# Sparse attention and a routed feed-forward on one Trainium2 core: blank rows ahead of the experts' lists instead of behind them

## The chip, the cores and the metric

The kernel runs on one core of one Trainium2 chip. The metric is device microseconds of one execution. A core has five engines with queues of their own: TensorE (PE; its weight loads appear as PEld), VectorE (DVE), ScalarE (ACT), GpSimd (POOL) and SyncE (SP), which here only starts transfers. Semaphores order them.

## What is computed

4096 tokens of 512 features pass through graph attention with a sparse adjacency and then through a mixture of 8 experts, of which each token uses two:

```python
x = x + gnn(layernorm(x), adj, Wks, Wqs, Wvs, Wo)         # 8 heads of 64, masked by adj

def ffn(xf):                                              # xf = layernorm(x)
    logits = xf @ Wg + bg                                 # 8 experts
    topk_scores, topk_idx = top_k(logits, 2)
    topk_w = softmax(topk_scores)
    h = gelu(einsum('nd,edh->neh', xf, W1) + b1)
    y = einsum('neh,ehf->nef', h, W2) + b2
    sel = take_along_axis(y, topk_idx[:, :, None], axis=1)
    return sum(topk_w[:, :, None] * sel, axis=1)

x = x + ffn(layernorm(x))
```

The kernel computes an expert only for the tokens that chose it.

## The kernel before

It has three stages.

- **Stage 1** normalizes the tokens, computes keys, values and queries, and reads the adjacency in 32 blocks of 2 MB to list each query tile's neighbours.
- **Stage 2** does the attention over the listed keys. As groups of query tiles finish, it routes their tokens: each token's row (512 features, its number, two gates and a mark) is scattered to two places of `xs_d` in device memory. Expert `e` has the rows from `e * R` on, where `R = N + P`.
- **Stage 3** goes through 71 tiles (`NB`) of 128 rows (`P`). A tile belongs to one expert.

An expert's list is rarely a multiple of 128 rows long, so its last tile reads beyond the end of the list. Before the change, 128 blank rows are written behind each list once its length is known. A blank row carries zero features, zero gates and the number of a spare output row, `N + p`, so whatever comes out of it goes to a spare row.

Between stages 2 and 3 stands the arithmetic that makes the tile table, followed by the blank writes:

```python
def finish_routing(pool, psum, blank):
    pn = psum.tile([P, E], F32, name="pn")
    nc.tensor.matmul(pn, ones, count, start=True, stop=True)     # tokens of each expert
    many = pool.tile([P, E], F32, name="many")
    nc.vector.tensor_copy(many, pn)
    # ... tiles of each expert, and their running sum
    nc.vector.tensor_tensor(past, ..., op=ALU.is_ge)             # [P, NB, E]
    nc.vector.tensor_reduce(expert, past, axis=AX.X, op=ALU.add)
    nc.vector.tensor_mul(past, past, ...)
    nc.vector.tensor_reduce(first, past, axis=AX.X, op=ALU.add)
    # ... first: the row of xs_d at which each tile begins
    nc.vector.tensor_add(many, many, start_e)                    # the end of each list
    nc.vector.tensor_copy(table[:, :NB], expert[:1])
    nc.vector.tensor_copy(table[:, NB : 2 * NB], first[:1])
    nc.vector.tensor_copy(table[:, 2 * NB :], many[:1])
    nc.vector.tensor_add(first, first, number.to_broadcast([P, NB]))

    nc.sync.dma_start(out=xs_d[E * R : E * R + P, :], in_=blank)
    for e in range(E):
        last = nc.values_load(table[:, 2 * NB + e : ...], engines=(SP,), ...)
        s = nc.sync.dma_start(out=xs_d[bass.ds(last, P), :], in_=blank)
        # ... declared free of order against the scatters
```

Then comes a branch, taken past a slower general path that these inputs do not need (`again > 0` runs it). Behind the branch, stage 3 fetches the rows of a tile and the two bias rows of its expert, and works in a software pipeline:

```python
again = nc.values_load(redo, ...)
with tc.If(again > 0):
    ...                                                          # the general path

def fetch(b):
    e = nc.values_load(table[:, b : b + 1], engines=(SP, PE), ...)
    f = nc.values_load(table[:, NB + b : NB + b + 1], engines=(SP,), ...)
    r = work.tile([P, W], F32, tag="row", bufs=5)
    nc.sync.dma_start(out=r, in_=xs_d[bass.ds(f, P), :])
    bb = work.tile([P, 2, D], F32, tag="bb", bufs=4)             # b1 and b2, broadcast

def second(b):
    gate = ...                                                   # from the row's mark and gates
    # py = hT @ w2 on TensorE
    nc.vector.tensor_add(y, py, bs[b][:, 1])
    nc.scalar.mul(y, y, gate[:, 1:2])
    nc.gpsimd.indirect_dma_start(                                # adds y to rows of out
        out=out, out_offset=IndirectOffsetOnAxis(ap=r[:, D : D + 1].bitcast(I32), axis=0),
        in_=y, in_offset=None, compute_op=ALU.add)

for b in range(NB):
    if b + 4 < NB: fetch(b + 4)
    turn_hidden(b)          # PE transposes into pht
    hidden(b + 1)           # ph = xT @ w1, + b1, gelu
    turn(b + 2)             # PE transposes into pt_e
    second(b)
```

All 8 experts' `w1` and `w2` are in on-chip memory before stage 3 needs them. `w1` comes in during stage 2, `w2` in eight loads of 1 MB at its end.

Of the kernel before, what the change touches and what calls it, by code (L numbers as in the profile page):

```python
# [10 lines left out]
F32 = mybir.dt.float32  # L11
BF16 = mybir.dt.bfloat16
I32 = mybir.dt.int32
AF = mybir.ActivationFunctionType
ALU = mybir.AluOpType
AX = mybir.AxisListType
PSUM = bass.MemoryType.PSUM
DRAM = bass.MemoryType.DRAM

P = 128  # L20
# [12 lines left out]
def kernel(  # L33
# [31 lines left out]
    nc = tc.nc  # L65
    N, D = x.shape
    H, KD = Wo.shape[0], Wo.shape[1]
    E, _, HID = W1.shape
# [8 lines left out]
    SP, PE = mybir.EngineType.SP, mybir.EngineType.PE  # L77
    DIAG = math.exp(IDENTITY_BIAS)
    LOW, HIGH = 1e-25, 1e37
    R = N + P  # L80
    NB = (2 * N + E * (P - 1)) // P
# [5 lines left out]
    const = ctx.enter_context(tc.tile_pool(name="const", bufs=1))  # L87
# [5 lines left out]
    xs_d = dram.tile([E * R + P, W], F32, name="xs_d")  # L93
# [9 lines left out]
        out=below, in_=ones, pattern=[[1, P]], compare_op=ALU.is_gt, fill=0.0,  # L103
        base=0, channel_multiplier=-1,
    )
    number = const.tile([P, 1], F32, name="number")
    nc.gpsimd.iota(number, pattern=[[0, 1]], base=0, channel_multiplier=1,
                   allow_small_or_imprecise_dtypes=True)
# [13 lines left out]
    for r in range(1, 4):  # L122
        nc.vector.tensor_add(gather4, gather4, ident[:, r * Q4 : r * Q4 + E])
    start_e = const.tile([P, E], F32, name="start_e")
    nc.gpsimd.iota(start_e, pattern=[[R, E]], base=0, channel_multiplier=0,
                   allow_small_or_imprecise_dtypes=True)
    before = const.tile([P, E, E], F32, name="before")
    nc.vector.memset(before, 0.0)
    for e in range(1, E):
# [6 lines left out]
                   allow_small_or_imprecise_dtypes=True)  # L136
# [4 lines left out]
                   allow_small_or_imprecise_dtypes=True)  # L141
    full = const.tile([P, NT], F32, name="full")
    nc.gpsimd.iota(full, pattern=[[P, NT]], base=0, channel_multiplier=0,
                   allow_small_or_imprecise_dtypes=True)
    first = const.tile([P, NB], F32, name="first")
    table = const.tile([1, 2 * NB + E], I32, name="table")
    redo = const.tile([1, 1], I32, name="redo")
    blank = const.tile([P, W], F32, name="blank")
    nc.vector.memset(blank, 0.0)
    nc.gpsimd.iota(blank[:, D : D + 1].bitcast(I32), pattern=[[0, 1]], base=N,  # L150
                   channel_multiplier=1)
# [77 lines left out]
    ap = ap_cm.__enter__()  # L229
    with tc.tile_pool(name="wqkv", bufs=1) as wp, tc.tile_pool(name="p1", bufs=3) as work, tc.tile_pool(  # L230
        name="p1b", bufs=2
    ) as block, tc.tile_pool(name="lists", bufs=2) as lp, tc.tile_pool(
        name="ps1t", bufs=2, space=PSUM
    ) as ps_t, tc.tile_pool(name="ps1", bufs=3, space=PSUM) as ps, tc.tile_pool(
        name="ps1a", bufs=1, space=PSUM
    ) as ps_a, tc.tile_pool(
        name="ps1l", bufs=2, space=PSUM
# [11 lines left out]
        for n, src, queue in (("k", Wks, nc.scalar), ("v", Wvs, nc.scalar), ("q", Wqs, nc.sync)):  # L249
            for c in range(DC):  # L250
                queue.dma_start(out=w[n][:, c], in_=src[ts(c, P), :])
        nc.sync.dma_start(
            out=wo, in_=Wo.rearrange("h k o -> (h k) o").rearrange("(c p) o -> p c o", p=P)
# [9 lines left out]
            out=step, in_=ones, pattern=[[1, P]], compare_op=ALU.is_equal, fill=0.0,  # L263
            base=-1, channel_multiplier=-1,
        )

        other = lp.tile([P, NT], F32, bufs=1, name="other")
        part = lp.tile([P, NT], F32, bufs=1, name="part")
        nc.gpsimd.affine_select(
            out=other, in_=one_f, pattern=[[-P // NT, NT]], compare_op=ALU.is_ge,  # L270
# [3 lines left out]
            out=part, in_=one_f, pattern=[[P // NT, NT]], compare_op=ALU.is_gt,  # L274
# [4 lines left out]
                       allow_small_or_imprecise_dtypes=True)  # L279
        slot_of = lp.tile([P, NT], F32, bufs=1, name="slot_of")  # L280
        nc.gpsimd.iota(slot_of, pattern=[[P, NT]], base=P, channel_multiplier=1,
                       allow_small_or_imprecise_dtypes=True)
# [15 lines left out]
        adj_in, flags, base, row_x, started, rows_of = {}, {}, {}, {}, {}, {}  # L298
# [199 lines left out]
            load_x1(TPB + t)  # L498
        list_constants()
        nc.sync.dma_start(out=out[N : N + P, :], in_=blank[:, :D])  # L500

# [11 lines left out]
        for u in range(8 * NTB + 1):  # L515
            b, s = divmod(u, 8)
# [146 lines left out]
    scatters = []  # L663
# [10 lines left out]

    why = "computed from counts that sum to 2 N"

    def finish_routing(pool, psum, blank):

        pn = psum.tile([P, E], F32, name="pn")
        nc.tensor.matmul(pn, ones, count, start=True, stop=True)  # L680
        many = pool.tile([P, E], F32, name="many")
        nc.vector.tensor_copy(many, pn)
        more = pool.tile([P, E, NT], F32, name="more")
        nc.vector.tensor_tensor(
            more, many.unsqueeze(2).to_broadcast([P, E, NT]),
            full.unsqueeze(1).to_broadcast([P, E, NT]), op=ALU.is_gt,
        )
        tiles_e = pool.tile([P, E], F32, name="tiles_e")
        nc.vector.tensor_reduce(tiles_e, more, axis=AX.X, op=ALU.add)
        none = pool.tile([P, E], F32, name="none")  # L690
        nc.vector.memset(none, 0.0)
        upto = pool.tile([P, E], F32, name="upto_e")
        nc.vector.tensor_tensor_scan(
            upto, tiles_e, none, initial=0.0, op0=ALU.add, op1=ALU.add
        )
        past = pool.tile([P, NB, E], F32, name="past_e")
        nc.vector.tensor_tensor(
            past, nth.unsqueeze(2).to_broadcast([P, NB, E]),
            upto.unsqueeze(1).to_broadcast([P, NB, E]), op=ALU.is_ge,
        )  # L700
        expert = pool.tile([P, NB], F32, name="expert")
        nc.vector.tensor_reduce(expert, past, axis=AX.X, op=ALU.add)
        nc.vector.tensor_mul(past, past, tiles_e.unsqueeze(1).to_broadcast([P, NB, E]))
        nc.vector.tensor_reduce(first, past, axis=AX.X, op=ALU.add)
        nc.vector.tensor_sub(first, nth, first)
        nc.vector.tensor_scalar_mul(first, first, float(P))
        nc.vector.scalar_tensor_tensor(
            first, expert, float(R), first, op0=ALU.mult, op1=ALU.add
        )
        nc.vector.tensor_scalar_min(first, first, float(E * R))  # L710
        nc.vector.tensor_scalar_min(expert, expert, float(E - 1))
        nc.vector.tensor_add(many, many, start_e)
        nc.vector.tensor_copy(table[:, :NB], expert[:1])
        nc.vector.tensor_copy(table[:, NB : 2 * NB], first[:1])
        nc.vector.tensor_copy(table[:, 2 * NB :], many[:1])
        nc.vector.tensor_add(first, first, number.to_broadcast([P, NB]))

        nc.sync.dma_start(out=xs_d[E * R : E * R + P, :], in_=blank)
        for e in range(E):
            last = nc.values_load(  # L720
                table[:, 2 * NB + e : 2 * NB + e + 1], engines=(SP,), min_val=e * R,
                max_val=e * R + N, skip_runtime_bounds_check_because=why,
            )
            s = nc.sync.dma_start(out=xs_d[bass.ds(last, P), :], in_=blank)
            for t in scatters:
                tc.declare_no_dep(s.ins, t.ins, reason="other rows")
            scatters.append(s)


    w1_cm = tc.tile_pool(name="w1", bufs=1)  # L730
# [3 lines left out]
    with tc.tile_pool(name="p2a", bufs=2) as two, tc.tile_pool(  # L734
        name="p2o", bufs=1
    ) as single, tc.tile_pool(name="p3", bufs=2) as small, tc.tile_pool(
        name="ps_s", bufs=3, space=PSUM
    ) as ps_s, tc.tile_pool(name="ps_o", bufs=1, space=PSUM) as ps_o, tc.tile_pool(
        name="ps_k", bufs=1, space=PSUM
    ) as ps_k, tc.tile_pool(name="ps_e", bufs=2, space=PSUM) as ps_e:  # L740
        work_cm = tc.tile_pool(name="p2", bufs=4)
        work = work_cm.__enter__()
# [236 lines left out]
        for n, (i, c) in enumerate(items):  # L979
# [7 lines left out]
            if n >= 56 and n % 7 == 0 and loads:  # L987
                e, d = loads.pop(0)
# [43 lines left out]
        nc.tensor.matmul(pf[:1], least, ones32[:, :1], start=True, stop=True)  # L1032
        nc.vector.tensor_copy(redo, pf[:1])

    with tc.tile_pool(name="end", bufs=1) as pool, tc.tile_pool(
        name="ps_end", bufs=1, space=PSUM
    ) as psum:
        finish_routing(pool, psum, blank)


    again = nc.values_load(
        redo, min_val=0, max_val=P, skip_runtime_bounds_check_because="counts partitions"
    )
    with tc.If(again > 0):
# [108 lines left out]
        with tc.tile_pool(name="g4", bufs=1) as pool, tc.tile_pool(  # L1153
            name="g4p", bufs=1, space=PSUM
        ) as psum:
            finish_routing(pool, psum, blank)


    with tc.tile_pool(name="p4", bufs=2) as work, tc.tile_pool(
        name="ps_x", bufs=2, space=PSUM  # L1160
    ) as ps_x, tc.tile_pool(name="ps_h", bufs=2, space=PSUM) as ps_h, tc.tile_pool(
        name="ps_t", bufs=2, space=PSUM
    ) as ps_t, tc.tile_pool(name="ps_y", bufs=2, space=PSUM) as ps_y:
        rows, es, xTs, bs, hs, hTs = {}, {}, {}, {}, {}, {}

        def fetch(b):
# [41 lines left out]
        def second(b):  # L1208
            r = rows[b]
            gate = work.tile([P, 2], F32, tag="gate", name=f"gate_{b}")  # L1210
            nc.vector.tensor_tensor(
                gate[:, 0:1], r[:, D + 3 : D + 4], first[:, b : b + 1], op=ALU.is_equal
            )
            nc.vector.scalar_tensor_tensor(
                gate[:, 1:2], r[:, D + 2 : D + 3], gate[:, 0:1], r[:, D + 1 : D + 2],
                op0=ALU.mult, op1=ALU.add,
            )
            py = ps_y.tile([P, D], F32, tag="y", name=f"py_{b}")
            for c in range(HC):
                nc.tensor.matmul(  # L1220
                    py, hTs[b][:, c, :], w2[:, bass.ds(es[b], 1), c, :],
                    start=(c == 0), stop=(c == HC - 1),
                )
            y = work.tile([P, D], F32, tag="y", bufs=3, name=f"y_{b}")
            nc.vector.tensor_add(y, py, bs[b][:, 1])  # L1225
            nc.scalar.mul(y, y, gate[:, 1:2])  # L1226
            nc.gpsimd.indirect_dma_start(  # L1227
                out=out,
                out_offset=bass.IndirectOffsetOnAxis(
                    ap=r[:, D : D + 1].bitcast(I32), axis=0  # L1230
                ),
                in_=y, in_offset=None, compute_op=ALU.add,
            )

# [57 lines left out]
```

## Time and profile before

| | before |
|---|---|
| time, median of 3 runs | 2406.32 us (2400.07 to 2424.73) |
| the profiled execution | 2258.89 us |
| its span, first to last instruction | 2257.2 us |
| mean granted TensorE clock | 0.967 |
| busy: PE, DVE, ACT, POOL | 2104.6, 1550.2, 966.7, 1252.9 us |
| moved by transfers | 494.85 MB, mean 219 GB/s |
| stage 3 (first row transposes to the end) | 1691.0 to 2257.2 us |

Times inside the profile count from its first instruction. In a timeline, a line gives start, duration, engine, source line, operation, destination and source; brackets give the idle time before it and what released it. "SPq" is the SyncE queue. In the table of waits, the figures behind the colon are total us, number of times and longest. A wait for several semaphores is put down to the one that came last by the profile. PEclk is the clock that TensorE was granted, as a share of full speed.

### The profile page before, as it was taken

Reading aid. Unit: us, or ns where it says so; the run is one execution under the profiler, and the core shown is the slowest. Engines: PE = TensorE matmul, PEld = TensorE weight load, DVE = VectorE, ACT = ScalarE, POOL = GpSimd, SP = SyncE. Lnnn points to the kernel's source line nnn. Section 1 sums busy time; section 2 is a strip of 40 time slices with the busy share of each in tenths; the row PEclk is TensorE's granted clock in tenths of the full one; section 3 lists DMA queues with packets and bytes.
Section 4 is the critical chain, followed back from the end, with each engine's and each line's share of the span. In section 5 each row is a group of like instructions: output and inputs, shape, how many; then the busy total and the mean of one; then the engine's idle time right before and its main releaser. Section 6 shows DMA issues by size and latency. Waiting matters only on the chain. (4 is left out here: it accounts for less than half of the span.)

```text
span 2257.2 us, 51565 instructions
## 1 busy us (share of the span) xinstructions
PE 2104.6 (93%) x20304; PEld 1404.5 (62%) x20304; DVE 1550.2 (69%) x2300; ACT 966.7 (43%) x1834; POOL 1252.9 (56%) x943
## 2 busy tenths in 40 slices
PE   7788887989999999999999999999839999999998
PEld 3344443478888788787777887777724444444443
DVE  4888778279999888898888889888842332323332
ACT  2222221256666556566565565656412222222221
POOL 1467766668887687677686767778511121121121
PEclk9999998999999999999999999999969999999999
DMA  7768989577787788778787877767576566556654
GB/s 287 288 228 298 316 302 314 171 235 245 249 266 244 218 259 264 222 245 262 211 277 235 259 230 227 252 197 231 170 253 137 131 140 140 132 140 137 135 135 89
DMA packets 215031, 494.85 MB, mean 219 GB/s; under 512 B 27345, under 2 KB 81873, under 8 KB 210690
## 3 DMA queue, kind: packets, MB, share of 16 engines
q0 software_dynamic: 79232, 249.68, 37.6%
q1 hardware_dynamic: 134402, 239.71, 33.7%
q8 instruction: 165, 2.70, 0.5%
q10 hardware_dynamic: 1152, 2.10, 0.3%
q14 instruction: 80, 0.66, 0.1%
HBM read 410.95 MB, written 80.44 MB: 218 GB/s over the span
## 5 line engine op out<-in xcount | busy, mean ns | idle before, releaser
L199 POOL DMA_INDIRECT kv<-kv_d,key_of x363 | 514.2, 1417 | 211.2 <-PE po L829 117.3
L817 DVE TENSOR_TENSOR e<-e,mask 128x1024 f32<-128x1024 f32 x363 | 444.0, 1224 | 88.2 <-ACT e L810 87.1
L835 DVE TENSOR_TENSOR acc<-acc,e 128x1024 f32<-128x1024 f32 x363 | 442.9, 1220 | 0.0
L810 ACT ACTIVATE e<-s 128x512 f32<-128x512 f32 x726 | 394.6, 596 | 98.4 <-PE s L800 94.5
L800 PE MATMUL s<-q,kT 64*128 64x128 f32 x5808 | 411.4, 281 | 5.1 <-ACT acc L810 5.1
L829 PE MATMUL po<-e,kv 128*64 128x128 f32 x5808 | 399.5, 280 | 0.0
L1227 POOL DMA_INDIRECT out_dram<-y,r x71 | 110.6, 1558 | 471.8 <-ACT y L1226 432.2
L800 PEld LDWEIGHTS s<-q,kT 64*128 64x128 f32 x5808 | 363.2, 191 | 5.4 <-ACT acc L810 5.4
L787 ACT COPY kT<-pk 128x512 f32<-128x512 f32 x395 | 232.0, 587 | 263.0 <-PE pk L784 258.3
L829 PEld LDWEIGHTS po<-e,kv 128*64 128x64 f32 x5808 | 311.6, 137 | 44.4 <-issue 1.0
L199 POOL DMA_INDIRECT mask<-in_adjT_dram,mask_of x230 | 283.5, 1233 | 70.1 <-issue 55.5
L1191 PE MATMUL ph<-w,xT 128*128 x568 | 257.8, 596 | 0.7 <-ACT xT L182 0.7
L1220 PE MATMUL py<-w,hT 128*128 x568 | 255.6, 593 | 0.9 <-DVE hT L1205 0.9
L1225 DVE TENSOR_TENSOR y<-py,bb 128x512 f32<-128x512 f32 x71 | 49.1, 692 | 225.6 <-PE py L1220 225.6
L784 PE MATMUL pk<-ident,kv 64*128 64x64 f32 x2904 | 169.6, 236 | 15.3 <-ACT kT L787 14.7
L309 DVE TENSOR_REDUCE flags<-adjT 128x32 f32<-128x4096 f32 x32 | 141.2, 4412 | 58.7 <-DMA adjT<-in_adjT_dram 58.6
L366 POOL TENSOR_SCALAR started<-slots,base 128x1152 bf16<-128x1152 f32 (+11 forms) x32 | 126.5, 3952 | 97.9 <-DVE longer L337 86.4
L784 PEld LDWEIGHTS pk<-ident,kv 64*128 64x128 f32 x2904 | 119.9, 139 | 91.9 <-issue 63.5
L199 POOL DMA_INDIRECT pm<-in_adjT_dram,mask_of x133 | 128.1, 963 | 79.0 <-DMA packed_d<-pm 47.5
L1191 PEld LDWEIGHTS ph<-w,xT 128*128 128x128 f32 x568 | 103.1, 192 | 103.7 <-issue 102.6
L1220 PEld LDWEIGHTS py<-w,hT 128*128 128x128 f32 x568 | 102.5, 190 | 104.0 <-issue 102.8
L1196 DVE TENSOR_TENSOR h<-ph,bb 128x512 f32<-128x512 f32 x71 | 49.1, 692 | 138.8 <-PE ph L1191 138.8
(577 smaller groups left out, 2338.3 us busy)
## 6 DMA issues: line engine op xcount, KB each, us to landing
adjT<-in_adjT_dram SPq DMA_DIRECT2D x32, 2048.0 KB
bb<-in_L_ffn_b_dram SPq DMA_DIRECT2D x142, 256.0 KB
r<-xs_d SPq DMA_DIRECT2D x71, 258.0 KB
kv_d<-kv SPq DMA_DIRECT2D x32, 512.0 KB
packed_d<-pm SPq DMA_DIRECT2D x133, 64.0 KB
mask<-packed_d SPq DMA_DIRECT2D x133, 64.0 KB
xt<-in_x_dram SPq DMA_DIRECT2D x32, 256.0 KB
qT_d<-qT SPq DMA_DIRECT2D x8, 1024.0 KB
```

The source lines that it names most:

```text
L199: nc.gpsimd.indirect_dma_start(out=to, out_offset=None, in_=src, in_offset=bass.IndirectOffsetOnAxis(ap=of[:, at[i] + c : at[i] + c + 1], ...
L309: nc.vector.tensor_reduce(flags[g][:, j, :], adj_in.pop(i), axis=AX.X, op=ALU.max)
L366: nc.gpsimd.tensor_scalar(started[i], slots[:, :n], base[g][:, j : j + 1], None, op0=ALU.is_ge)
L784: nc.tensor.transpose(pk[:, r, ts(p, KD)], kv[n][half, ts(p, P)], ident[half, half])
L787: nc.scalar.copy(kT[n].rearrange("k p (r j) -> k r p j", r=2), pk[:, :, : NP * KD].rearrange("k r (p j) -> k r p j", p=NP),)
L800: nc.tensor.matmul(s[r][:, p, :], k[rows, p, :], q_in[i][rows, p, :], start=True, stop=True,)
L810: nc.scalar.activation(e[:, r * NP : (r + 1) * NP], s[r], AF.Exp)
L817: nc.vector.tensor_mul(e, e, m.unsqueeze(1).to_broadcast([P, 2 * NP, P]))
L829: nc.tensor.matmul(po[i][r * KD : (r + 1) * KD, p, :], v[:, ts(h, KD)], e[:, r * NP + p, :], start=(c < 0 and p == 0), stop=(c == listed[i ...
L835: nc.vector.tensor_add(acc[i], acc[i], e)
L1191: nc.tensor.matmul(ph, xTs[b][:, c, :], w1[:, bass.ds(es[b], 1), c, :], start=(c == 0), stop=(c == DC - 1),)
L1220: nc.tensor.matmul(py, hTs[b][:, c, :], w2[:, bass.ds(es[b], 1), c, :], start=(c == 0), stop=(c == HC - 1),)
```

## The change

The blank rows move from behind each list to ahead of it, where their place does not depend on any count: the lists now begin at `e * R + 128`, and nine blank blocks are written once, at the start of stage 1. An expert's last tile no longer reads beyond the end of its list. It begins further up, so that it ends with the list, and so it reads again some rows that belong to the tile before it (or, where a list is shorter than 128, blank rows). Those rows are computed a second time. Their results must not be added twice, so each row of a tile is marked as its own or not (`mine`), and rows that are not its own are sent to the spare output rows by a number worked out per tile (`to`). Besides, the memory of several pools is taken over tile by tile instead of all at once (`reuse_waits="tile"`).

```diff
-    nc.gpsimd.iota(start_e, pattern=[[R, E]], base=0, ...)
+    nc.gpsimd.iota(start_e, pattern=[[R, E]], base=P, ...)
...
-    table = const.tile([1, 2 * NB + E], I32, name="table")
+    table = const.tile([1, 2 * NB], I32, name="table")
...
+    mine = const.tile([P, NB], F32, name="mine")
+    spare = const.tile([P, 1], F32, name="spare")      # N + partition
...
         nc.sync.dma_start(out=out[N : N + P, :], in_=blank[:, :D])
+        for e in range(E + 1):
+            nc.sync.dma_start(out=xs_d[e * R : e * R + P, :], in_=blank)
...
         nc.vector.tensor_reduce(expert, past, axis=AX.X, op=ALU.add)
+        end = pool.tile([P, E + 1], F32, name="end")
+        nc.vector.memset(end[:, E:], float(E * R + P))
+        nc.vector.tensor_add(end[:, :E], many, start_e)
+        more_e = pool.tile([P, E], F32, name="more_e")
+        nc.vector.tensor_sub(more_e, end[:, 1:], end[:, :E])
+        ends = pool.tile([P, NB, E], F32, name="ends")
+        nc.vector.tensor_mul(ends, past, more_e.unsqueeze(1).to_broadcast([P, NB, E]))
+        till = pool.tile([P, NB], F32, name="till")
+        nc.vector.tensor_reduce(till, ends, axis=AX.X, op=ALU.add)
...
+        nc.vector.tensor_scalar(till, till, end[:, 0:1], -float(P), op0=ALU.add, op1=ALU.add)
+        begin = pool.tile([P, NB], F32, name="begin")
+        nc.vector.tensor_tensor(begin, first, till, op=ALU.min)
...
-        nc.vector.tensor_add(many, many, start_e)
         nc.vector.tensor_copy(table[:, :NB], expert[:1])
-        nc.vector.tensor_copy(table[:, NB : 2 * NB], first[:1])
-        nc.vector.tensor_copy(table[:, 2 * NB :], many[:1])
-        nc.vector.tensor_add(first, first, number.to_broadcast([P, NB]))
-
-        nc.sync.dma_start(out=xs_d[E * R : E * R + P, :], in_=blank)
-        for e in range(E):
-            last = nc.values_load(table[:, 2 * NB + e : ...], engines=(SP,), ...)
-            s = nc.sync.dma_start(out=xs_d[bass.ds(last, P), :], in_=blank)
-            ...
+        nc.vector.tensor_copy(table[:, NB:], begin[:1])
+        nc.vector.tensor_add(begin, begin, number.to_broadcast([P, NB]))
+        nc.vector.tensor_tensor(mine, begin, first, op=ALU.is_ge)
+        nc.vector.tensor_copy(first, begin)
...
-    with tc.tile_pool(name="end", bufs=1) as pool, tc.tile_pool(
-        name="ps_end", bufs=1, space=PSUM
+    with tc.tile_pool(name="end", bufs=1, reuse_waits="tile") as pool, tc.tile_pool(
+        name="ps_end", bufs=1, space=PSUM, reuse_waits="tile"
     ) as psum:
...      (and reuse_waits="tile" on the five pools of stage 3)
...
+            to = work.tile([P, 2], F32, tag="to", bufs=3, name=f"to_{b}")
+            nc.vector.scalar_tensor_tensor(
+                to[:, 0:1], r[:, D : D + 1].bitcast(I32), spare, mine[:, b : b + 1],
+                op0=ALU.subtract, op1=ALU.mult,
+            )
+            nc.vector.tensor_add(to[:, 1:2].bitcast(I32), to[:, 0:1], spare)
             nc.gpsimd.indirect_dma_start(
                 out=out,
-                out_offset=IndirectOffsetOnAxis(ap=r[:, D : D + 1].bitcast(I32), axis=0),
+                out_offset=IndirectOffsetOnAxis(ap=to[:, 1:2].bitcast(I32), axis=0),
                 in_=y, in_offset=None, compute_op=ALU.add,
             )
```

More of the change, by code (lines that the diff above doesn't have):

```diff
@@ L124 @@
     start_e = const.tile([P, E], F32, name="start_e")
-    nc.gpsimd.iota(start_e, pattern=[[R, E]], base=0, channel_multiplier=0,
+    nc.gpsimd.iota(start_e, pattern=[[R, E]], base=P, channel_multiplier=0,
                    allow_small_or_imprecise_dtypes=True)
@@ L145 @@
     first = const.tile([P, NB], F32, name="first")
-    table = const.tile([1, 2 * NB + E], I32, name="table")
+    table = const.tile([1, 2 * NB], I32, name="table")
     redo = const.tile([1, 1], I32, name="redo")
+    mine = const.tile([P, NB], F32, name="mine")
+    spare = const.tile([P, 1], F32, name="spare")
+    nc.gpsimd.iota(spare, pattern=[[0, 1]], base=N, channel_multiplier=1,
+                   allow_small_or_imprecise_dtypes=True)
     blank = const.tile([P, W], F32, name="blank")
@@ L675, with finish_routing @@
     why = "computed from counts that sum to 2 N"
-    def finish_routing(pool, psum, blank):
+    def finish_routing(pool, psum):
         pn = psum.tile([P, E], F32, name="pn")
@@ L705, in finish_routing @@
         nc.vector.tensor_sub(first, nth, first)
-        nc.vector.tensor_scalar_mul(first, first, float(P))
+        nc.vector.tensor_scalar(first, first, float(P), float(P), op0=ALU.mult, op1=ALU.add)
         nc.vector.scalar_tensor_tensor(
@@ L710, in finish_routing @@
         nc.vector.tensor_scalar_min(first, first, float(E * R))
+        nc.vector.tensor_scalar(till, till, end[:, 0:1], -float(P), op0=ALU.add, op1=ALU.add)
+        begin = pool.tile([P, NB], F32, name="begin")
+        nc.vector.tensor_tensor(begin, first, till, op=ALU.min)
         nc.vector.tensor_scalar_min(expert, expert, float(E - 1))
-        nc.vector.tensor_add(many, many, start_e)
         nc.vector.tensor_copy(table[:, :NB], expert[:1])
-        nc.vector.tensor_copy(table[:, NB : 2 * NB], first[:1])
-        nc.vector.tensor_copy(table[:, 2 * NB :], many[:1])
-        nc.vector.tensor_add(first, first, number.to_broadcast([P, NB]))
-        nc.sync.dma_start(out=xs_d[E * R : E * R + P, :], in_=blank)
-        for e in range(E):
[L720 to L727, printed above, removed]
+        nc.vector.tensor_copy(table[:, NB:], begin[:1])
+        nc.vector.tensor_add(begin, begin, number.to_broadcast([P, NB]))
+        nc.vector.tensor_tensor(mine, begin, first, op=ALU.is_ge)
+        nc.vector.tensor_copy(first, begin)
     w1_cm = tc.tile_pool(name="w1", bufs=1)
@@ L1033 @@
         nc.vector.tensor_copy(redo, pf[:1])
-    with tc.tile_pool(name="end", bufs=1) as pool, tc.tile_pool(
-        name="ps_end", bufs=1, space=PSUM
+    with tc.tile_pool(name="end", bufs=1, reuse_waits="tile") as pool, tc.tile_pool(
+        name="ps_end", bufs=1, space=PSUM, reuse_waits="tile"
     ) as psum:
-        finish_routing(pool, psum, blank)
+        finish_routing(pool, psum)
     again = nc.values_load(
@@ L1155 @@
         ) as psum:
[L1156 to L1163, printed above, removed]
+            finish_routing(pool, psum)
+    with tc.tile_pool(name="p4", bufs=2, reuse_waits="tile") as work, tc.tile_pool(
+        name="ps_x", bufs=2, space=PSUM, reuse_waits="tile"
+    ) as ps_x, tc.tile_pool(
+        name="ps_h", bufs=2, space=PSUM, reuse_waits="tile"
+    ) as ps_h, tc.tile_pool(
+        name="ps_t", bufs=2, space=PSUM, reuse_waits="tile"
+    ) as ps_t, tc.tile_pool(name="ps_y", bufs=2, space=PSUM, reuse_waits="tile") as ps_y:
         rows, es, xTs, bs, hs, hTs = {}, {}, {}, {}, {}, {}
@@ L1226, in second @@
             nc.scalar.mul(y, y, gate[:, 1:2])
+            to = work.tile([P, 2], F32, tag="to", bufs=3, name=f"to_{b}")
[4 more added lines that the diff above has]
+            nc.vector.tensor_add(to[:, 1:2].bitcast(I32), to[:, 0:1], spare)
             nc.gpsimd.indirect_dma_start(
                 out=out,
-                out_offset=bass.IndirectOffsetOnAxis(
-                    ap=r[:, D : D + 1].bitcast(I32), axis=0
-                ),
+                out_offset=bass.IndirectOffsetOnAxis(ap=to[:, 1:2].bitcast(I32), axis=0),
                 in_=y, in_offset=None, compute_op=ALU.add,
```

## The prediction

> **What bounds the kernel now.** I read in this order: the engines' shares on the page, a table of engine load by stretch, TensorE's waits in the expert stage, then the timelines of VectorE and of the SyncE queue around the seam between attention and experts. The page gives PE 93% of the span. The change does not touch TensorE's work, so the question is where PE stands still and whether the change reaches those places. The table of busy time by stretch, after the header `us, PE busy (x) PEld busy (x) DVE busy (x) ACT busy (x) POOL busy (x), PEclk, DMA share, GB/s`:
>
> ```profile
> 1642.00:1672.00 30.00, 13.72 (x70) 7.81 (x70) 13.64 (x89) 4.05 (x13) 7.76 (x8) 0.62 0.98 358
> 1672.00:1691.00 19.00, 0.01 (x1) 0.04 (x1) 5.65 (x20) 0.00 (x0) 0.00 (x0) 0.50 0.45 157
> 1691.00:1707.00 16.00, 12.40 (x34) 6.20 (x35) 2.74 (x7) 3.67 (x5) 0.00 (x0) 0.82 0.91 185
> 1707.00:2249.00 542.00, 540.86 (x1671) 266.10 (x1669) 165.08 (x349) 127.60 (x208) 109.05 (x70) 1.00 0.59 131
> ```
>
> From 1707 to 2249 us, PE is busy 540.86 of 542 us at full clock: the expert loop is bound by its matmuls, and nothing that other engines gain or lose there shows. From 1672 to 1691 PE does nothing. PE's waits from 1690 us to the end confirm it:
>
> ```profile
> PE pt_e L181 <- DMA bb<-in_L_ffn_b_dram: 25.4, 1, 25.4
> PE pt_e L181 <- DMA r<-xs_d: 2.9, 1, 2.9
> PE py L1220 <- DVE hT L1205: 0.9, 1, 0.9
> PE ph L1191 <- ACT xT L182: 0.7, 1, 0.7
> ```
>
> One wait of 25.4 us (the profile names `bb`, but the row tile `r` lands at the same moment), and four others of 4.5 us in all. What holds the 25.4 us stands in VectorE's timeline (start, duration, then the idle time before it in brackets):
>
> ```profile
> 1666.88 0.16 DVE L659 TENSOR_TENSOR rows<-more,rows 128x1 f32<-128x1 f32 x1
> 1673.05 0.17 DVE L682 COPY many<-pn 128x8 f32<-128x8 f32 x1 [6.01 <-DMA out_dram<-xr]
> ...
> 1675.93 0.75 DVE L703 TENSOR_TENSOR past_e<-past_e,tiles_e 128x568 f32<-128x568 f32 x1
> 1676.71 0.74 DVE L704 TENSOR_REDUCE first<-past_e 128x71 f32<-128x568 f32 x1
> ...
> 1678.60 0.18 DVE L713 CAST table<-expert 1x71 int32<-1x71 f32 x1
> ```
>
> and in the SyncE queue's:
>
> ```profile
> 1674.30 0.36 SPq L718 DMA_DIRECT2D xs_d<-blank  x1
> 1675.43 6.84 SPq L724 DMA_DIRECT2D xs_d<-blank  x8
> 1687.85 0.38 SPq L1177 DMA_DIRECT2D r<-xs_d  x1
> ```
>
> VectorE starts the closing arithmetic of the routing 6.01 us late, released by a store to `out` that it does not read; a new pool takes over memory. The tile table is ready at 1678.78, yet the first row tile is asked for only at 1687.85: SyncE issues nine blank writes until 1682.2, then passes the branch and its landings. The branch itself, from the instructions of its line:
>
> ```profile
> L1044 SPq EVENT_SEMAPHORE  x9: 17/17/17, 1686.1 to 1686.7; - x9
> L1044 SPq COMPARE_BRANCH  x1: 50/50/50, 1682.7 to 1682.7; - x1
> ```
>
> From 1682.7 to 1686.1 SyncE executes nothing: 3.4 us behind the branch.
>
> [...]Here the first 258 KB row tile takes 1690.96 - 1687.85 = 3.1 us to first use; I use the trace's figure. [...]clock 0.50 in the gap, and the first eight `ph` matmuls take 5.71 us against 3.60 later.[...]
>
> **The change part by part.**
>
> (a) *Tile-wise reuse waits on the closing pools.* In the changed program's instruction order, `many<-pn` waits for TensorE alone, no longer for two transfer queues. `pn` was ready by 1665.45 + 0.19. VectorE is busy with the last group until 1667.04, so the chain begins about 1667.05: **6.0 us earlier**.
>
> (b) *More arithmetic on that chain.* Before, it takes 1678.78 - 1673.05 = 5.73 us. Two wide operations join (`ends`, `till`), each 128x568 like L703 and L704, which start 1676.71 - 1675.93 = 0.78 us apart: 1.56 us. Four narrow ones (`end`, `more_e`, the shift of `till`, `begin`) at the 0.1 to 0.25 us pitch of their neighbours, less one removed cast, make about 0.4 us. New length 7.7 us, table ready at 1667.05 + 7.7 = **1674.7**, 4.0 us earlier. The conversion of `first` behind the table costs the loop nothing.
>
> (c) *Blank writes leave the seam.* Nothing is left for SyncE between the last attention store (issued by 1661.1) and the branch. It passes the branch about 1666.4, as PE does; [...]the landings it must await end at about 1673 (the store that released VectorE at 1673.05). All beside VectorE's chain. The token scatters into `xs_d` have landed by 1674.25, because the first blank write waited on them until then. So the table, at 1674.7, comes last, narrowly. From the cast to the issue, I take 1.0 us (`many` cast end 1674.40 to first L724 at 1675.43) to 1.3 us: first row tile at about 1675.9, landing 3.1 us later at 1679.0. TensorE now starts at 1679.0 instead of 1690.99: **12.0 us earlier**. Of these 12.0 us, 4.0 are the table and 8.0 the blank writes and what stood behind them.
>
> (d) *Second weights.* They might still be under way when the loop starts earlier. Their eight loads are issued by 1657.6; the stretch to 1672 moves 358 GB/s, then the rate falls to 157. They have landed by about 1672, and the first `py` would come 15 us after the start, near 1694. No wait.
>
> (e) *Blank writes at the start of stage 1.* Nine writes of 258 KB, 2.3 MB, now stand ahead of the first adjacency block on the SyncE queue. At the page's first-slice rate of 287 GB/s that is 8.1 us. VectorE's flags reduction needs the block:
>
> ```profile
> 26.78 4.42 DVE L309 TENSOR_REDUCE flags<-adjT 128x32 f32<-128x4096 f32 x1 [5.36 <-DMA adjT<-in_adjT_dram]
> 31.12 0.69 DVE L156 BATCH_NORM_STATS2 stats_a<-xt 128x6 f32<-128x512 f32 x1
> 38.61 4.42 DVE L309 TENSOR_REDUCE flags<-adjT 128x32 f32<-128x4096 f32 x1 [4.16 <-DMA adjT<-in_adjT_dram]
> 53.40 4.42 DVE L309 TENSOR_REDUCE flags<-adjT 128x32 f32<-128x4096 f32 x1 [10.37 <-DMA adjT<-in_adjT_dram]
> ```
>
> The first reduction slips from 26.8 to about 35, the second from 38.6 to about 43, and the third had 10.37 us of idle time before it, so the delay is gone by 53 us. Until then TensorE runs projections without a gap (10 of 10 us busy from 20 to 60), and the next thing that it needs from VectorE is the second block's statistics for the transposes at 53.03, which would now be ready about 43. Cost 0; I allow 0.5 us.
>
> (f) *Two narrow operations more per tile* on VectorE, about 0.16 + 0.24 = 0.4 us, 71 times 28 us. VectorE is busy 165 of 542 us there, TensorE is full: nothing on the path. Row tiles are also freed without waiting for the scatter; TensorE never waited for those in the loop except once at its start (the 2.9 us[...]), which stays.
>
> Sum: -12.0 + 0.5 = **-11.5 us**. The profiled execution takes 2258.9 us and the timed ones a median of 2406.3; nothing in the trace says where the 147 us between them lie. The gap consists of transfers and narrow VectorE work, so I carry the saving over in microseconds: 2406.3 - 11.5 = **2394.8 us**, 0.5%.
>
> **The rivals.** *The scatters or SyncE take the place of the table.* For: they are within a microsecond or two of it (1674.25, 1673). If the last scatter or the branch lands 3 us later, 9 us remain. Against: weights and stores have drained by then. Time about 2397. *The early blank writes cost what the late ones gave back.* For: DMA is above 100% busy at 10 to 20 us[...]. Against: the 10 us of slack above. If I am wrong, all 8 us return, as stage 1 loads VectorE and DMA heavily later (0.64 to 0.93 of the DMA engines): about 2402. *The timed execution has waits in the loop that the profiled one lacks.* If row tiles come late there, freeing them before the scatter lands removes waits in 71 tiles; half a microsecond each would make another 35 us, about 2360. Only the 147 us speak for it; the trace shows PE full. *The whole 25 us gap goes*: it can't, since about 12 us of arithmetic and 4 us of issue and landing remain.
>
> **Range and chances.** The mechanism gives -4 to -15 us. The three times of before spread over 24.7 us, more than the effect, so the range is mostly that spread: 2376 to 2408. A gain of 2% would need 48 us, beyond the whole gap; a loss of 2% would need a stall that nothing here suggests. Faster by over 2%: 0.02; within: 0.97; slower: 0.01.
>
> **What would show it.** In the profile after: `many` follows the last `rows` within 0.1 us; the table's last cast ends near 1674.7; no blank write there; the first row tile is asked for near 1676 and TensorE starts near 1679 (both plus any shift of stage 1); the first transposes of the second block still near 53 us; the loop still full, 7.7 us per tile; `pt_e` waits 13 to 14 us, not 25.4. Wrong if stage 1 ends later by several microseconds, or if TensorE's first wait is put down to the scatters at over 16 us.

## The result and the profile after

The changed kernel takes 2536.30 us (median of six, 2528.66 to 2543.27) against 2411.05 us for the kernel before: ratio **1.0515**, 95% interval 1.0473 to 1.0557. I had predicted 2394.8 us. It is 125 us slower.

One remark on comparing: the attention stage, which the change leaves alone, ends near 1670 us in some profiles and near 1800 us in others, of the kernel before as well as of the changed ones, and alike within each of the three sets of experiments below (the kernel before takes 2390 us on the chip of the first set, 2259 and 2260 us on those of the two others; why is open). So times are compared only as ratios within a set, and stages by their lengths; times such as 2380 or 2500 us in the expected texts assume the 2390 us of the first set.

Busy time by stretch, changed kernel (the same columns as for the kernel before):

```profile
1783.00:1813.00 30.00, 17.11 (x149) 10.75 (x148) 20.31 (x106) 7.72 (x19) 6.79 (x7) 0.80 0.76 270
1813.00:1828.00 15.00, 0.08 (x1) 0.11 (x2) 7.51 (x25) 0.00 (x0) 1.94 (x2) 0.50 0.65 234
1828.00:1845.00 17.00, 14.77 (x38) 7.15 (x39) 3.22 (x13) 4.18 (x6) 0.00 (x0) 0.79 0.65 180
1845.00:2527.00 682.00, 586.25 (x1667) 274.48 (x1665) 180.75 (x483) 128.86 (x207) 109.03 (x70) 0.95 0.47 104
```

The seam did become shorter: TensorE idles about 15 us, not 24. But the loop of stage 3, with the same matmuls, now takes 682 us where the same part took 542, and TensorE is busy in only 86% of it. TensorE's longest waits from 1800 us to the end name what it lacks:

```profile
PE pht L1214 <- ACT h L1208: 88.8, 46, 3.8
PE pt_e L185 <- DMA r<-xs_d: 18.1, 2, 16.5
PE py L1231 <- DVE hT L1216: 6.8, 6, 2.7
```

46 waits for the hidden activations. ScalarE waits for them in turn on VectorE (first line, from ScalarE's waits), and VectorE's waits in stage 3 begin with the second:

```profile
ACT h L1208 <- DVE h L1207: 221.9, 68, 7.8
DVE to L1240 <- DMA out_dram<-y,to: 414.4, 68, 7.9
```

In 68 of 71 tiles VectorE stands up to 7.9 us in front of `to`, the new tile of row numbers, until a scatter into `out` has landed. VectorE's timeline over one tile of the changed kernel:

```profile
2101.28 0.22 DVE L1225 SCALAR_TENSOR_TENSOR gate<-r,gate 128x1 f32<-128x1 f32 x1
2107.46 0.22 DVE L1240 SCALAR_TENSOR_TENSOR to<-r,spare,mine 128x1 f32<-128x1 int32 x1 [5.95 <-DMA out_dram<-y,to]
2107.71 0.16 DVE L1244 TENSOR_TENSOR to<-to,spare 128x1 int32<-128x1 f32 x1
2107.79 0.69 DVE L1207 TENSOR_TENSOR h<-ph,bb 128x512 f32<-128x512 f32 x1
2108.40 0.68 DVE L1236 TENSOR_TENSOR y<-py,bb 128x512 f32<-128x512 f32 x1
```

A 0.22 us operation waits 5.95 us, and behind it stand `h`, which the next tile's matmuls need, and `y`, which the next scatter needs. The chain of waits, over the tile that follows, shows the circle closed:

```profile
2109.39 0.71 ACT y L1237
2110.11 0.27 issue
2110.37 7.80 DMA out_dram<-y,to
...
2118.20 0.23 DVE to L1240
...
2119.14 0.69 DVE y L1236
```

`to` waits for the scatter of one tile earlier, `y` stands behind `to`, ScalarE scales `y`, and the next scatter goes out. From this chain and the lines around it: 6.6 to 7.8 us until the scatter has landed, 0.9 from the start of `to` to `y`, 1.7 to 2.0 through `y` and its scaling to the next scatter. The scatters start 9.3 to 10.5 us apart. TensorE needs 542 / 70 = 7.74 per tile in the kernel before.

### The profile page after: what moved, and what is told of

Same layout as the page of the kernel before. It is cut to its first block, busy times and chain, and to the rows that moved or that the text cites. A ratio compares the mean times of both kernels' runs of the same rounds, so it can differ in the third digit from the quotient of the medians.

```text
span 2535.2 us, 51683 instructions
## 1 busy us (share of the span) xinstructions
PE 2235.0 (88%) x20304; PEld 1466.4 (58%) x20304; DVE 1564.2 (62%) x2449; ACT 963.1 (38%) x1834; POOL 1229.2 (48%) x944
## 5 line engine op out<-in xcount | busy, mean ns | idle before, releaser
L203 POOL DMA_INDIRECT kv<-kv_d,key_of x363 | 486.7, 1341 | 380.9 <-PE po L838 245.2
L809 PE MATMUL s<-q,kT 64*128 64x128 f32 x5808 | 449.3, 288 | 10.0 <-issue 7.3
L838 PE MATMUL po<-e,kv 128*64 128x128 f32 x5808 | 412.1, 283 | 7.6 <-issue 7.1
L1245 POOL DMA_INDIRECT out_dram<-y,to x71 | 110.6, 1557 | 604.2 <-ACT y L1237 604.2
L809 PEld LDWEIGHTS s<-q,kT 64*128 64x128 f32 x5808 | 391.5, 196 | 18.3 <-issue 11.8
L203 POOL DMA_INDIRECT mask<-in_adjT_dram,mask_of x230 | 291.5, 1267 | 72.8 <-issue 65.2
L1202 PE MATMUL ph<-w,xT 128*128 x568 | 289.2, 656 | 0.7 <-ACT xT L186 0.7
L1240 DVE SCALAR_TENSOR_TENSOR to<-r,spare,mine 128x1 f32<-128x1 int32 x71 | 15.6, 219 | 417.6 <-DMA out_dram<-y,to 414.4
L1202 PEld LDWEIGHTS ph<-w,xT 128*128 128x128 f32 x568 | 113.3, 210 | 124.9 <-issue 119.9
L186 ACT COPY xT<-pt_e 128x512 f32<-128x512 f32 x71 | 41.4, 583 | 291.0 <-PE pt_e L185 291.0
```

Of the source, the lines that this page charges most:

```text
L203: nc.gpsimd.indirect_dma_start(out=to, out_offset=None, in_=src, in_offset=bass.IndirectOffsetOnAxis(ap=of[:, at[i] + c : at[i] + c + 1], ...
L809: nc.tensor.matmul(s[r][:, p, :], k[rows, p, :], q_in[i][rows, p, :], start=True, stop=True,)
L838: nc.tensor.matmul(po[i][r * KD : (r + 1) * KD, p, :], v[:, ts(h, KD)], e[:, r * NP + p, :], start=(c < 0 and p == 0), stop=(c == listed[i ...
L1202: nc.tensor.matmul(ph, xTs[b][:, c, :], w1[:, bass.ds(es[b], 1), c, :], start=(c == 0), stop=(c == DC - 1),)
```

## The experiments

Theory A: `to` has only three buffers, so its next writing waits for a scatter that still reads it, and the operations behind it on VectorE wait with it (above, `h` and `y` start 0.33 and 0.94 us after `to`). Rival B: the scatters themselves go slower, through rows that go to the spare rows. Rival C: the early blank rows slow the attention. Rival D: the tile-wise memory reuse disturbed the loop. The ratio is to the kernel before in the same set; the loop is from the first row transpose to the end of the profile.

| run | ratio (95% interval) | loop, us |
|---|---|---|
| kernel before again | 1.0013 (0.9995 to 1.0031) | 563.1 |
| changed kernel | 1.0515 (1.0473 to 1.0557) | 707.3 |
| 4 buffers for `to` | 1.0478 (1.0446 to 1.0509) | 686.4 |
| kernel before plus `to` | 1.0529 (1.0490 to 1.0568) | 699.1 |
| changed, plain pools in stage 3 | 1.0495 (1.0463 to 1.0526) | 690.5 |
| 5 buffers | 1.0295 (1.0272 to 1.0317) | 637.3 |
| 6 buffers | 0.9969 (0.9956 to 0.9982) | 564.2 |
| 8 buffers | 0.9958 (0.9946 to 0.9971) | 565.1 |
| 3 buffers, program order | 0.9957 (0.9944 to 0.9969) | 565.6 |
| 8 buffers, plain closing pools | 0.9994 (0.9983 to 1.0006) | 563.4 |
| before, tile-wise closing pools | 0.9998 (0.9989 to 1.0006) | 566.1 |
| 8 buffers, short chain | 0.9952 (0.9935 to 0.9970) | 564.7 |

**The kernel before, again.**

> The kernel before, unchanged, for a second profile beside those of the changed kernels. Its first profile spans 2257 us while its timed executions lie at 2400 to 2425. Theory A (the loop of stage 3 carries the whole loss): the attention stage of this profile ends near 1800 us instead of 1665, as it does in the changed kernel, and stage 3 still takes about 566 us. Rival C (the early blank rows slow the attention): the attention stage ends near 1665 us again and the timed executions lose their time elsewhere. Time by both: 2411 us.

Its attention ended at 1794.6 us (last routing operation) and its loop took 2386.4 - 1823.3 = 563.1 us, against 707.3 in the changed kernel. In the same set the attention ended at 1792.3 and 1802.5 us with early blank rows (4 buffers; plain pools in stage 3) and at 1799.4 us with late ones (before plus `to`). Rival C falls: the attention is as long without early blank rows, and the loop carries the loss. The loop is also as full here as in the first profile of before (537.06 of 538 us), so this profile shows none of the waits that the prediction's third rival looked for in the timed executions. Of the 147 us between that first profile and the times of before, which I had left open, 129 lie between the two profiles, nearly all of it (127.6) in the attention stage; that the timed executions had the long stage too fits, but no profile of them shows it.

**One part of the change alone: `to` in the kernel before.**

```diff
+            to = work.tile([P, 2], F32, tag="to", bufs=3, name=f"to_{b}")
+            nc.vector.scalar_tensor_tensor(to[:, 0:1], r[:, D : D + 1].bitcast(I32), spare, mine[:, b : b + 1], ...)
+            nc.vector.tensor_add(to[:, 1:2].bitcast(I32), to[:, 0:1], spare)
-                    ap=r[:, D : D + 1].bitcast(I32), axis=0
+                out_offset=IndirectOffsetOnAxis(ap=to[:, 1:2].bitcast(I32), axis=0),
```

> The kernel before with one part of the change alone: the two narrow VectorE operations per tile that put the scatter's row numbers into a tile of their own with three buffers (all rows count as own, so the numbers are the same as before; blank rows, table and pools are those of before). Theory A: stage 3 takes about 705 us instead of 566, the time is about 2411 + 140 = 2550 us. Rival B (rows computed twice and sent to spare rows) and rival D (tile-wise reuse): about 2411 us, as neither is in this kernel.

Measured 1.0529. No row is computed twice here, no row number differs from the kernel before, no pool is reused tile-wise, and the whole loss is there. The first line of VectorE's waits in stage 3:

```profile
DVE to L1233 <- DMA out_dram<-y,to: 406.4, 67, 8.0
```

Rivals B and D fall as causes of the loss. Rival D was also tried directly, by taking `reuse_waits="tile"` from the five pools of stage 3:

> The changed kernel without the tile-wise memory reuse on the five pools of stage 3 (the closing pools keep it). Theory A: the wait for the scatters is still there, 2530 to 2545 us. Rival D (tile-wise reuse changed the loop): stage 3 back at 566 us, about 2400 us. Rival B: 2536 us.

1.0495: the loss stays.

**More buffers.** `bufs=3` becomes 4, then 5, 6 and 8, nothing else.

> The changed kernel with four buffers for the tile of scatter numbers instead of three. Theory A (VectorE, in program order, waits at each tile for the landing of a scatter issued one tile before, because the number tile has only three buffers): the waited-for scatter is one tile older, 7.7 us more slack against a landing of about 7 us, so the wait disappears, stage 3 takes about 566 us, and the time is about 2400 us. Rival B (the scatters themselves are slower, or rows sent to the spare rows hold them up): another buffer only delays the wait by one tile, about 2530 us. Rival D (tile-wise memory reuse changed the loop's order): 2536 us, unchanged.

1.0478. My expectation by theory A failed here, and rivals B and D seemed to gain. The built order, in which the scheduler placed each engine's instructions, told why. With three buffers, `to(b+2)` stands ahead of `y(b)` and needs the scatter of tile b-1. With four, the scheduler put the arithmetic a tile further ahead: `to(b+3)` stands there, and a buffer four tiles older is again that of tile b-1. VectorE's waits agree:

```profile
DVE to L1240 <- DMA out_dram<-y,to: 400.5, 67, 7.1
```

So I changed the theory to A2: what counts is how far back the scatter lies for which VectorE is made to wait at a given place (rival A in the texts below is the plain form, that there are too few buffers). The next two runs differ in that alone, one tile.

> The changed kernel with five buffers for the tile of scatter numbers. With four, the scheduler put the number arithmetic one tile further ahead, so that it still waited for the same scatter (issued after y(b-1), asked for before y(b)). With five the built order again asks, ahead of y(b), for the landing of the scatter of tile b-1. Theory A2 (it is the distance between the scatter waited for and the place of the wait in VectorE's order that counts, not the number of buffers): still slow, a tile takes 9.2 us, time about 2500 us. Rival A (buffers as such): about 2380. Rival B (the scatters cannot go faster, e.g. for rows sent to spare rows): 2500.

> The changed kernel with six buffers: one more than the last, and VectorE's order is the same, but ahead of y(b) it now asks for the scatter of tile b-2, issued one tile period (7.7 us) earlier, against a landing of 6.5 to 8 us. Theory A2: the wait disappears, stage 3 takes about 563 us as in the kernel before, time about 2380 us. Rival B: about 2500.

In five buffers the wait ahead of `y(b)` is for scatter b-1, in six for b-2, with the same order of operations. Measured: 1.0295 and 0.9969. With five the waits for the scatters still add up to 396.0 us (66 times); with six none of VectorE's waits in stage 3 is for a scatter (`to` now waits for its row tile instead, 69 times, which lands before `y` is due and costs nothing: TensorE is busy in 537.06 of 538 us of the loop). The expected size was off for five buffers: the loss is 3%, not 5, as a tile takes 637.3 / 71 = 9.0 us against 707.3 / 71 = 10.0 with three. Here `h` stands ahead of the wait in VectorE's order and only `hT`, the copy of the transposed activations, behind it: TensorE waits for `hT`, 58 times and 50.2 us in all from 1790 us to the end, but never longer than 1.9 us, and its mean clock over the whole profile is 0.971, not below the 0.965 to 0.970 of the kernel before in this set. With eight:

> The changed kernel with eight buffers: no wait of the number arithmetic on any scatter that y does not await itself. Theory A2: as with six buffers, about 2377 us: the kernel before (2390 on this chip) less what the shorter seam brings (28.7 us from the last routing operation to the first row transpose in the kernel before, 15.2 in the changed one). Rival B: about 2500.

0.9958, and the loop's stretch is full as it was in the kernel before (538 us of the loop, busy time by engine):

```profile
1705.00:2243.00 538.00, 537.06 (x1662) 264.63 (x1661) 188.41 (x479) 126.99 (x207) 109.02 (x70) 1.00 0.60 132
```

**Three buffers, another order.** The loop under `tc.manual_schedule()`, which keeps the order of the program.

> The changed kernel with three buffers as it is, but stage 3 kept in the order of the program instead of the scheduler's: the number arithmetic of tile b now stands behind y(b) on VectorE, where the scatter of tile b-3 landed long ago. Theory A2: the wait disappears with three buffers, stage 3 about 563 us, time 2375 to 2385 us, unless the program's order costs something elsewhere. Rival A (three buffers are too few) and rival B: about 2505 us.

0.9957, with three buffers. VectorE's timeline in this run:

```profile
2102.68 0.69 DVE L1236 TENSOR_TENSOR y<-py,bb 128x512 f32<-128x512 f32 x1 [2.80 <-PE py L1231]
2103.29 0.21 DVE L1240 SCALAR_TENSOR_TENSOR to<-r,spare,mine 128x1 f32<-128x1 int32 x1
2103.53 0.16 DVE L1244 TENSOR_TENSOR to<-to,spare 128x1 int32<-128x1 f32 x1
```

`to` stands behind `y` and waits for nothing. The same two operations, the same three buffers, the same scatters: the place in the queue made the loss. Program order also moves other operations (`gate` now stands ahead of `y`), but five and six buffers differ in the one wait alone and show the same. Theory A2 holds.

**What the seam gains, and by which part.** The gap is counted from the end of the last routing operation on VectorE to TensorE's first row transpose. With eight buffers, the closing pools as before (`reuse_waits="tile"` taken from `end` and `ps_end`):

> The changed kernel with eight buffers, but with the two closing pools taken over all at once as in the kernel before (blank rows stay early). What the seam gains by each part: theory S (the release of VectorE's chain is a part of its own): many waits again for the last store to out, 6 to 11 us, and the gap from the last routing operation to the first row transpose grows from 15.3 us to 21 to 26 us; ratio to the kernel before 0.998 to 1.000 instead of 0.996. Rival S2 (the early blank rows carry the gain, the chain hides behind weights and branch): gap stays at 15 to 18 us, ratio 0.996 to 0.997.

The kernel before with only that added to its closing pools:

> The kernel before with tile-wise reuse on the two closing pools alone. Theory S with both parts needed: the table is ready 6 to 11 us earlier, but the blank writes, which wait for the scatters, and the branch behind them still stand before the first row tile: the gap shrinks by 0 to 5 us from 24 to 29 us, ratio 0.998 to 1.000. Rival S3 (the pools alone carry the gain): gap about 15 to 17 us, ratio 0.996.

| closing pools | blank rows late | blank rows early |
|---|---|---|
| taken over at once | 24.0 (28.7 in the second profile, 23.7 with `to`) | 21.1 |
| tile by tile | 25.3 | 14.9 |

The gap of one and the same kernel differs by up to 5 us between profiles, as `many` waits 6 to 11.6 us for the last store, so only the 14.9 stands clearly apart. By the times, each part alone makes no measurable difference (0.9998, interval 0.9989 to 1.0006, and 0.9994, interval 0.9983 to 1.0006); together they bring 0.9958. Without tile-wise reuse, VectorE waits as long as before, here 5.98 us and released by SyncE at the branch (L1053), and with early blank rows its chain is what comes last:

```profile
1679.94 0.17 DVE L688 COPY many<-pn 128x8 f32<-128x8 f32 x1 [5.98 <-SPq L1053]
```

With tile-wise reuse but late blank rows, the chain is 6 us earlier, and SyncE's queue holds the end instead: the blank writes wait for the scatters until 1678.57, and the last is issued at 1679.71 + 6.79 = 1686.5.

```profile
1678.57 0.36 SPq L718 DMA_DIRECT2D xs_d<-blank  x1
1679.71 6.79 SPq L724 DMA_DIRECT2D xs_d<-blank  x8
```

Last, with eight buffers, the three operations on `begin`, `mine` and `first` were moved behind the branch:

> The changed kernel with eight buffers, and with the three operations on begin, mine and first that the table does not need moved behind the branch. The first row tile is asked for only after VectorE has passed its own branch, 3 us after its last operation, so if this is what comes last in the seam, 0.75 us less work before the branch starts the loop 0.75 us earlier: gap 14.5 us instead of 15.2, ratio about 0.9955. If the landings of the second weights come last, the gap stays at 15.2 us or above.

The gap is 14.5 us, as expected, against 14.9 to 15.3 us in the six other profiles of the same seam; one profile is little to go by, and 0.9952 cannot be told from 0.9958 by time. Short chain, eight buffers and program order all beat the kernel before, by 0.4 to 0.5%.

## Why the prediction was wrong, step by step

**(f), two narrow operations per tile, is the step that failed.** It said "nothing on the path" because VectorE is busy 165 of 542 us and TensorE is full; the opening reading, that nothing other engines lose in the loop shows, has the same fault. The busy time was right (180.75 us now), but an engine with room can still be made to stand. `to` is read by the scatter until it has landed, so writing it again is a wait, and the built order, which I had before me, showed that wait ahead of `y(b)`. I counted durations there and not waits. Measured: 707.3 - 563.1 = +144 us. About 96 us of it are TensorE's waits (88.8 + 6.8). The rest, 48.5 us, is longer busy time for the same 1704 matmuls: 601.2 us, against 552.7 in the second profile of before. About 30 us of that goes with a slower clock: 18 groups of eight matmuls take 4.6 to 5.4 us where 3.6 is usual, the granted clock is 0.50 for about 3.4 us at each of them, and the mean clock of the loop is 0.95 against 0.99. The other 18 us are not explained by these groups; that matmuls which no longer run back to back are recorded as longer is my reading, and not shown. Of the 18 slow groups, 15 follow a wait of 1.9 to 2.9 us and three a wait of 3.5 to 3.8 us, while other waits of up to 2.6 us left the clock at 1.00: in this loop the length of a wait alone does not tell whether a slow group follows.

**(a), the earlier start of the chain**, was right: `many` follows the last `rows` at once (they start at 1812.73 and 1812.66).

**(b), 7.7 us of arithmetic**: 7.25 measured, 1812.73 to 1819.98.

**(c), the seam**: 12.0 us predicted; 24.0 - 14.9 = 9.1 measured with eight buffers against the profile that the prediction read, and up to 13.8 against the second profile of before. From the last cast to the first row tile's issue I had taken 1.0 to 1.3 us; it is 1825.20 - 1819.98 = 5.2. The piece that I missed is in the branch lines of the changed kernel:

```profile
L1053 SPq EVENT_SEMAPHORE  x8: 17/17/17, 1817.9 to 1823.5; - x8
L1053 DVEq COMPARE_BRANCH  x1: 72/72/72, 1821.2 to 1821.2; - x1
L1053 DVEq EVENT_SEMAPHORE  x1: 21/21/21, 1824.3 to 1824.3; - x1
```

SyncE reads the table only at 1824.4, 4.4 us behind the last cast to the table: after VectorE has passed its own branch, and after the semaphore instructions of its own branch line, the last at 1823.5. Its waits name the one that came last:

```profile
SPq L1183 <- DVEq L1053: 0.9, 1, 0.9
```

With four buffers, where SyncE's own instructions ended earlier, the same wait is 5.2 us. I had let SyncE's branch run beside the chain, which it does, and had forgotten VectorE's, which follows it. In the kernel before, it was hidden behind the blank writes: VectorE was past its branch at 1682.8 us, SyncE at 1686.1.

**(d), the second weights**: they cost the first `py` nothing, as predicted. But they took longer than the prediction said: it had them landed 5 us after the last routing operation, while in the changed kernel the transfers run at 402 GB/s until 7 us after it and fall to 17 GB/s only 9 us after it. SyncE's semaphore instructions at the branch, which I take for the wait for these landings (no view names it), ended within a microsecond of what came last.

**(e), early blank rows**: right. First reductions of stage 1 in the changed kernel:

```profile
34.52 4.42 DVE L313 TENSOR_REDUCE flags<-adjT 128x32 f32<-128x4096 f32 x1 [12.75 <-DMA adjT<-in_adjT_dram]
42.10 4.41 DVE L313 TENSOR_REDUCE flags<-adjT 128x32 f32<-128x4096 f32 x1
52.28 4.42 DVE L313 TENSOR_REDUCE flags<-adjT 128x32 f32<-128x4096 f32 x1 [5.76 <-DMA adjT<-in_adjT_dram]
```

35, 43 and 53 were predicted. SyncE issues the nine blank writes from 17.66 to 23.88 us and the first adjacency block at 23.92, where the kernel before issued it at 18.55. The slack took the delay up: in the two later sets the attention ends at 1665.0 to 1674.0 us with early blank rows (six profiles), and at 1669.5 with late ones.

**The sum.** Loop +144, and a seam shorter by 13.6 us against the second profile of before (28.7 to 15.1): +131 by the profiles, +125 by the times. (The two profiles as a whole differ by 149 us, as the attention ends 18 us later in the changed one; the profiles of one set, above, show no such shift by the change.) The prediction's opening also counts four other waits of 4.5 us beside the 25.4; its lines show three, with the same sum. With the loop mended, the rest of the prediction is left: -11.5 us predicted, and by the ratio 0.9958 of 2259 us about -9.5.

## What to carry to other kernels

Two tiny operations on an engine that is 70% idle cost 5%, because one of them overwrites what a transfer still reads (68 waits, 414.4 us in all) and stands ahead of work that others need: for each new operation, look up in the built order what it waits for and what is queued behind it, before adding up durations. Counting buffers is not enough where a scheduler decides the place, since it may use an added buffer to go further ahead and wait for the same transfer, as with four buffers here (1.0478); check which transfer is waited for, and how old it is at that place. And where two waits stand side by side, removing either one alone may gain nothing (here 0.9998 and 0.9994, both together 0.9958): count what comes last once it is gone.

## What was not expected of the hardware

- In the changed kernel, a scatter-add of 128 rows of 2 KB took 6.4 to 8.3 us (median 6.8) from its start on GpSimd until `to` could be written, in 67 of VectorE's 68 waits for it, and 4.8 us in one near the end. The first row tile, of nearly the same size, took 3.1 us by an ordinary load in the kernel before.
- At the branch past the general path, VectorE stands 2.8 to 3.7 us and TensorE's sequencer 6.2 to 6.9 us, in the 12 profiles that show the branch's line; SyncE stands 2.9 to 6.3 us, in which a wait for landings may be hidden (not shown).
- In the loop of the changed kernel the granted clock was 0.50 for about 3.4 us at each of 18 waits of 1.9 to 3.8 us, where matmuls of `ph`, once of `py`, were recorded at up to 1.2 us, most often 1.06, instead of 0.59, and it stayed at 1.00 at other waits of up to 2.6 us.
